# Output projection of chunk pairs by Strassen's seven products, in single steps spread over two iterations

## The chip, the cores and the metric

The kernel runs on one core of one Trainium2 chip. The metric is the device time of one execution in microseconds (us); lower is better. On the core, TensorE multiplies matrices (PE in the profile, its weight loads PEld), VectorE (DVE), ScalarE (ACT) and GpSimd (POOL) work on elements, and SyncE (SP) issues most of the transfers.

## The reference, cut to what matters

A layer on x of 2 x 1024 tokens with 512 columns, all in float32: an FFN with two experts (each token goes to one), an attention with a recurrent state of slots, and the same FFN again.

```python
x = x + 0.5 * _L0_ffn_ref(_layernorm(x), w_router, w_fc, w_proj)
x = x + _L0_attn_ref(_layernorm(x), Wq, Wk, Wv, Wg, Ws, Wo, g_norm_weight)
x = x + 0.5 * _L0_ffn_ref(_layernorm(x), w_router, w_fc, w_proj)

def _L0_attn_ref(hidden_states, ...):           # 16 heads, DK 64, DV 128, 64 slots
    q, k, v = (to_heads(hidden_states @ W) for W in (Wq, Wk, Wv))
    s = clip(to_heads(hidden_states @ Ws), -32, 32)
    o = _chunk_abc(q, k, v, s)                  # two scans over the tokens, softmax over slots between
    g = hidden_states @ Wg
    o = o * rsqrt(mean(o * o, -1) + 1e-5) * g_norm_weight
    o = o * (g * sigmoid(g))
    return o.reshape(b, t, 2048) @ Wo           # the output projection
```

## The kernel before

The first FFN (`Mixture`, `ffn`) sorts tokens by expert into blocks of up to 512 and runs six passes over them. The attention then runs as one loop over 64 units: two batches, four groups of four heads, eight chunks of 128 tokens, in this order from the outside in. The loop is a software pipeline: iteration i begins unit i (`cur`), does the softmax and the slot weights of unit i-1 (`mid`), and ends unit i-2 (`old`) with `transpose_out` and `project_out`. Even iterations begin an even chunk, odd ones an odd chunk. The last FFN's steps (`then_steps`) are drawn into the last iterations.

The order of TensorE's work in attention is fixed by hand: `on_pe` (L949 in the profile) makes each matmul issue behind the one before it. To have something to do while the softmax chain goes through VectorE and ScalarE, the loop calls `project` at set places; it takes steps of two generators, `values_gates` ("v") and `keys_slots` ("k"). These compute the projections of a pair of chunks together, by the seven products of Strassen's scheme (Winograd's form): four token sums X (`token_sums`) are made on VectorE, the weight sums were made beforehand on GpSimd (`weight_sums`, stored to HBM and loaded again by `load_values_gates` and `load_keys_slots`). A product is two matmuls of 128 x 128 by 256 or 512 columns; each float32 matmul has two records in the profile.

What the prediction speaks of, by name:

- Bp, svp, tk, ov, Ap, ok, ts, tu, `to` and skp are the PSUM tiles of a unit's own chain on TensorE: slot weights, state products, transposes of keys and slots, outputs, scores, slot scores, and the transposes around the softmax. B and A (L1106) are the masked copies of Bp and Ap that VectorE makes. CT is the running sum over slots (L1119) and rC its reciprocal (L1124). sq and ms lead to the norm's factor (L1208 to L1215), sg is the gate, and og the gated output. mx, e and rs are the softmax.
- `project_out` (tile `po`, L1261 for the add) multiplies a chunk's oT, four heads of 128 rows, by the group's 512 rows of Wo: four matmuls of 512 columns into one whole bank, then one VectorE add to the rows x.
- `keys_slots` has two tiles: kU (256 columns), and kV with halves C and V in one bank. kp, kv and ku are copies of partial sums to SBUF. It is drawn in five steps of two or one products.
- PSUM: tag `pj` has two buffers, for C and V of `values_gates`, for kU and kV, for the queries pq (made every fourth unit) and for po. Tag `st` is shared by ts, svp, skp, the rank's rp, and hC of the FFN. SBUF: all weights share the eleven buffers of `large_tile`, and sums the six of `sum_tile`.
- `feed` takes a finished row block into the last FFN's router. When enough have been fed it calls `rank` at once, which puts two small products (rp) on TensorE and scatters the rows.

Of the kernel before, what the change touches and what calls it, by code (L numbers as in the profile page):

```python
# [49 lines left out]
def tile_macaron(  # L50
# [55 lines left out]
    causal = const.tile([P, NPR, P], F32, tag="causal", name="causal")  # L106
    for h in range(NPR):
        nc.gpsimd.affine_select(
            out=causal[:, h, :],
            in_=ones,  # L110
            pattern=[[1, P]],
            compare_op=ALU.is_ge,
            fill=0.0,
            base=0,
            channel_multiplier=-1,
        )
# [4 lines left out]
    strict = const.tile([P, P], F32, tag="strict", name="strict")  # L121
    nc.gpsimd.tensor_tensor(strict, causal[:, 0, :], ident, ALU.subtract)
# [52 lines left out]
    vg_sums = [tc.dram_tile([P, 2 * 4 * 512], F32, name=f"vgs{g}") for g in range(NG)]  # L175
    ks_sums = [tc.dram_tile([P, 2 * 4 * 256], F32, name=f"kss{g}") for g in range(NG)]
# [8 lines left out]
    def layernorm_T(src, rows, xT, b, ph):  # L185
        for blk in range(2 * b, 2 * b + 2):
            xT[blk] = large_tile([P, DC, 512], f"xnT{ph}_{blk}")
            for j in range(4):
# [14 lines left out]
                nc.vector.tensor_scalar(xn, x, mv[:, 0:1], rstd, ALU.subtract, ALU.mult)  # L203
                tp = ps1.tile([P, DC, P], F32, tag="tr", name=f"ln{nm}")
# [27 lines left out]
    class Mixture:  # L232
# [3 lines left out]
        def __init__(self, ph, plan, split):  # L236
            self.ph, self.rows, self.split = ph, None, split
            self.passes, self.groups = plan
            self.starts = [sum(self.passes[:j]) for j in range(NPASS)]
            self.e1 = small_t([P, NT], "e1", f"e1{ph}")  # L240
            self.run = small_t([P, NT], "run", f"run{ph}")
            self.before = small_t([P, NT], "bef", f"bef{ph}")
            self.pos = small_t([P, NT], "pos", f"pos{ph}", mybir.dt.int32)

            self.own = small_t([P, NPASS], "own", f"own{ph}")
            self.seen = self.ranked = self.done = 0

        def feed(self):  # L250
# [12 lines left out]
            if self.seen == self.ranked + self.groups[self.done]:  # L263
                self.rank(self.groups[self.done])
                self.done += 1

        def rank(self, n):
# [14 lines left out]
            nc.tensor.matmul(rp[:, 0:n], lhsT=strict, rhs=e1[:, g], start=True, stop=False)  # L282
# [3 lines left out]
            V.tensor_tensor(r0, tokid[:, g], rp[:, 0:n], ALU.subtract)  # L286
            V.scalar_tensor_tensor(r1, rp[:, 0:n], float(REGION), r0, ALU.add, ALU.subtract)
# [164 lines left out]
    def ffn(m, views):  # L452
# [140 lines left out]
        def hidden_fast(ps, ck, xT, T, wfc, S, a, sums):  # L593
# [3 lines left out]
            for q in range(2):  # L597
# [18 lines left out]
                hA = work.tile([P, 512], F32, tag="oT", name=f"hA{nm}")  # L616
                hB = work.tile([P, 512], F32, tag="oT", name=f"hB{nm}")
# [216 lines left out]
    class Attention:  # L834
# [19 lines left out]
        def weight_sums(self):  # L854
# [18 lines left out]
            def load(j):  # L873
                g, d = j // 3, j % 3
                if d == 2:
                    return load_w(w_ks[g], f"kw{g}")
# [9 lines left out]
            for j in range(3 * NG):  # L886
                g, d = j // 3, j % 3
# [6 lines left out]
                else:  # L894
                    w = w.rearrange("p (k d n c) -> p k d n c", k=2, d=2, n=2)
                    parts = w[:, 0, :, 0], w[:, 0, :, 1], w[:, 1, :, 0], w[:, 1, :, 1]
                    to = ks_sums[g].rearrange("p (t d c) -> p t d c", t=4, d=2)
                    T = sum_tile([P, 3, 2, 256], f"K{g}")
                for i, _ in enumerate(sums(*parts, T)):
                    if i == 3:  # L900
                        store(to, T, parts[1])
                    if i == 1:
                        ahead = load(j + 1) if j != 2 and j + 1 < 3 * NG else None
# [18 lines left out]
        def load_keys_slots(self, b, g):  # L922
            nm = f"{b}_{g}"
            w = w_ks[g].rearrange("p (k d n c) -> p k d n c", k=2, d=2, n=2)
            B = sum_tile([P, 3, 2, 256], f"wks{nm}")
            for k in range(2):
                nc.sync.dma_start(out=B[:, k], in_=w[:, k, :, 0])
            T = large_tile([P, 4, 2, 256], f"ksT{nm}")
            nc.sync.dma_start(out=T, in_=ks_sums[g].rearrange("p (t d c) -> p t d c", t=4, d=2))
            nc.sync.dma_start(out=B[:, 2], in_=w[:, 1, :, 1])  # L930
            self.ks[b, g] = B[:, 0], B[:, 1], B[:, 2], T[:, 0], T[:, 1], T[:, 2], T[:, 3]
# [5 lines left out]
        def load_outputs(self, b, g):  # L937
            self.o[b, g] = load_w(w_o[g], f"wo{b}_{g}")

    def attention(att, then, then_steps, weight_steps):  # L940
# [83 lines left out]

        def keys_slots(u):
            pair = u, units[u.n + 1]
            B11, B21, B22, T1, T2, T3, T4 = att.ks[u.b, u.g]
            a11, a12, a21, a22 = halves(u)
            U = ps2.tile([P, 256], F32, tag="pj", name=f"kU{u.nm}")

            def keep(bank, tag):
                t = work.tile([P, 256], F32, tag=tag, name=f"{tag}{u.nm}", bufs=1)
                nc.scalar.copy(t, bank)
                return t
# [5 lines left out]
            def slot(v, bank, other):  # L1040
                v.E = work.tile([P, HG * M], F32, tag="E", name=f"E{v.nm}", bufs=3)
                nc.vector.tensor_tensor(v.E, bank, other, ALU.add)
                nc.vector.tensor_scalar(v.E, v.E, -32.0, 32.0, ALU.max, ALU.min)
                nc.scalar.activation(v.E, v.E, AF.Exp)

            product(U, a11, B11, True)
            p1 = keep(U, "kp")

            bank = ps2.tile([P, 2, 256], F32, tag="pj", name=f"kV{u.nm}")
            C, V = bank[:, 0], bank[:, 1]  # L1050
            product(C, a12, B21, True)
            nc.vector.tensor_tensor(key(u), C, p1, ALU.add)
            yield
            product(V, u.S[:, 0], T1, False)
            p5 = keep(V, "kv")
            product(U, u.S[:, 1], T2, False)
            u2 = keep(U, "ku")
            yield
            product(V, u.S[:, 3], B22, False)
            slot(u, V, u2)  # L1060
            yield
            product(U, u.S[:, 2], T3, False)
            slot(pair[1], U, p5)
            yield
            product(U, a22, T4, False)
            nc.scalar.copy(key(pair[1]), U)
            yield

# [24 lines left out]
        def masked_products(u, name, lT, rT):  # L1093
# [3 lines left out]
            for j in range(2):  # L1097
# [8 lines left out]
                nc.vector.tensor_tensor(m[:, ts(j, NPR), :], pp, causal[:, 0:NPR, :], ALU.mult)  # L1106
# [143 lines left out]
        def project_out(u):  # L1250

            tag = "at" if u.i >= NT - 3 and u.g == NG - 1 else "pj"
            pj = ps2.tile([P, D], F32, tag=tag, name=f"po{u.nm}")
            for h in range(HG):
                on_pe(
                    nc.tensor.matmul,
                    pj, lhsT=u.oT[:, h, :], rhs=att.o[u.b, u.g][:, ts(h, D)],
                    start=(h == 0), stop=(h == HG - 1),
                )
            x = rows[u.blk][:, u.c % 4, 0:D]  # L1260
            nc.vector.tensor_tensor(x, pj, x, ALU.add)  # L1261
            if u.g == NG - 1:
                then.feed()

# [16 lines left out]
        ahead = keys = None  # L1281
# [12 lines left out]
        for i in range(n + 2):  # L1294
            cur = units[i] if i < n else None
            mid = units[i - 1] if 1 <= i <= n else None
            old = units[i - 2] if i >= 2 else None


            def project(even, odd):  # L1300
                if i >= n - 1:
                    next(then_steps)
                for step in (odd if i % 2 else even) if cur else "":
                    if step == "v":
# [6 lines left out]
            project("k", "v")  # L1311
            if mid:
                slot_scores(mid)
            project("k", "v")
            if old:
                transpose_out(old)
            if mid:
                slot_softmax(mid)
            project("kvk", "v")
# [3 lines left out]
            project("vk", "v")  # L1323
# [7 lines left out]
            project("", "")  # L1331
            if cur and i % 2 == 0:
                ahead = None
            if mid:
# [3 lines left out]
                if mid.b == 0 and mid.c < 6 and mid.g < NG - 1:  # L1338
# [5 lines left out]
            if old:  # L1344
                project_out(old)
            if cur:
                if cur.g == NG - 1 and cur.b == 0:
                    next(norm)
                if cur.g == 0 and cur.b and cur.c in (1, 2):
                    att.load_rows(2 * cur.b + cur.c - 1)  # L1350

                if cur.c >= 4 and cur.n + NC < n:
# [7 lines left out]
                    else:  # L1360
                        att.load_outputs(v.b, v.g)
                if cur.g == NG - 1 and cur.b == B - 1:
                    if cur.c == 1:
                        then.lead_pass()
                    elif cur.c >= 3:

                        with tc.issue_after(mid.gated.ins):
                            next(then_steps)

# [9 lines left out]
    for ps, ck in ffn(first_mixture, x1_views):  # L1379
        if ps == NPASS - 1 and ck >= 2 and att.rows[ck - 2] is None:  # L1380
            att.load_rows(ck - 2)
        if ps == NPASS - 1 and ck == 3:
            with tc.issue_after(first_mixture.mark_dve.ins):
                next(norm, None)
            if (0, 0) not in att.vg:
# [3 lines left out]
        if ps == 2 and ck == 2:  # L1389
            for _ in range(min(3, 12 - done)):  # L1390
# [53 lines left out]
```

## Time and profile before

| What | us |
|---|---|
| median of 3 runs | 2368.47 |
| lowest and highest | 2363.77, 2371.63 |
| the profiled execution | 2368.13 |
| its span | 2366.4 |
| attention loop, from 535 to 1857 | 1322 |
| attention draining into the last FFN, 1857 to 1945 | 88 |

Each line of the profile's groups names the source line, the engine, the operation, the tile written and those read, the shape and count, then the busy time in us and the mean of one in ns, then the engine's idle time before them and what ended most of it. In the order of time a line has start and duration in us; matmuls of one kind in a row are merged. A matmul's record is about 0.17 us longer than the distance to the next one's start, since matmuls are pipelined; distances between starts are the better measure. Sums by stage list the window, its length, the busy time of PE, PEld, DVE, ACT and POOL with their counts, the granted TensorE clock as a share of full speed, and DMA.

### The profile page before, as it was taken

Reading aid. Unit: us, or ns where it says so; the run is one execution under the profiler, and the core shown is the slowest. Engines: PE = TensorE matmul, PEld = TensorE weight load, DVE = VectorE, ACT = ScalarE, POOL = GpSimd, SP = SyncE. Lnnn points to the kernel's source line nnn. Section 1 sums busy time; section 2 is a strip of 40 time slices with the busy share of each in tenths; the row PEclk is TensorE's granted clock in tenths of the full one; section 3 lists DMA queues with packets and bytes.
Section 4 is the critical chain, followed back from the end, with each engine's and each line's share of the span. In section 5 each row is a group of like instructions: output and inputs, shape, how many; then the busy total and the mean of one; then the engine's idle time right before and its main releaser. Section 6 shows DMA issues by size and latency. Waiting matters only on the chain.

```text
span 2366.4 us, 28341 instructions
## 1 busy us (share of the span) xinstructions
PE 2270.1 (96%) x10552; PEld 1566.4 (66%) x10552; DVE 1389.4 (59%) x3116; ACT 782.9 (33%) x1462; POOL 470.8 (20%) x401
## 2 busy tenths in 40 slices
PE   6999999999999999999999999999999989999998
PEld 5686787866656666665556666665665668888865
DVE  6553556557656656756666655655656666666411
ACT  2221222324334333343333343343433322222222
POOL 3613616101101101100101000000001244534000
PEclk9999999999999999999999999999999999999999
DMA  7516435221311411311301110111010104323442
GB/s 285 218 54 241 151 115 221 76 104 45 121 45 63 143 40 54 143 32 37 138 27 58 72 35 15 72 41 35 29 36 31 77 23 152 107 77 120 165 169 98
DMA packets 56938, 222.72 MB, mean 94 GB/s; under 512 B 5983, under 2 KB 13151, under 8 KB 38880
## 3 DMA queue, kind: packets, MB, share of 16 engines
q1 hardware_dynamic: 51232, 203.52, 24.1%
q0 software_dynamic: 5280, 16.85, 1.8%
q8 instruction: 84, 1.38, 0.2%
q14 instruction: 54, 0.44, 0.1%
q10 hardware_dynamic: 288, 0.52, 0.1%
HBM read 189.86 MB, written 31.54 MB: 94 GB/s over the span
## 4 chain that ended last, share of the span: by engine, by line
PE 75%; DVE 13%; issue 6%; ACT 2%; POOL 2%; DMA 1%; SPq 0%; POOLq 0%; DVEq 0%; ACTq 0%
PE U L949 9%; PE oa L673 6%; PE po L949 6%; PE hU L606 6%; PE pq L949 5%; PE o L673 5%; PE V L949 4%; PE kU L949 4%; PE hp L509 4%; PE kV L949 3%; PE hV L606 3%; PE op L728 3%; PE ov L949 3%; PE C L949 2%; DVE rC L1124 2%
## 5 line engine op out<-in xcount | busy, mean ns | idle before, releaser
L1217 POOL TENSOR_TENSOR sg<-sg,ms 128x512 f32<-128x512 f32 x64 | 67.6, 1056 | 1248.6 <-DVE ms L1215 1209.1
L949 PE MATMUL po<-wo,oT 128*128 128x512 f32 x512 | 238.4, 609 | 1.7 <-DVE A L1106 1.7
L949 PEld LDWEIGHTS po<-wo,oT 128*128 128x128 f32 x512 | 92.6, 191 | 102.4 <-issue 93.0
L509 PE MATMUL hp<-xsT,wfc 128*128 128x256 f32 (+1 forms) x768 | 149.8, 350 | 10.3 <-DMA wfc<-in_w_fc_dram 5.6
L509 PEld LDWEIGHTS hp<-xsT,wfc 128*128 128x128 f32 x768 | 128.0, 193 | 33.6 <-issue 13.9
L728 PE MATMUL op<-wp,a 128*128 128x512 f32 x320 | 143.2, 593 | 0.0
L1213 ACT ACT_TABLE_LOAD x64 | 82.1, 1283 | 157.1 <-DVE ms L1212 157.0
L496 DVE SCALAR_TENSOR_TENSOR t<-hp,r 128x256 f32<-128x256 f32 (+1 forms) x96 | 36.3, 378 | 153.7 <-ACT r L495 151.7
L949 PE MATMUL U<-vgT,X 128*128 128x512 f32 x256 | 120.3, 592 | 0.0
L949 PE MATMUL pq<-xnT,wq 128*128 128x512 f32 x256 | 112.5, 592 | 0.0
L1124 DVE RECIPROCAL rC<-CT 128x256 f32<-128x256 f32 x64 | 111.4, 1740 | 0.6
L606 PE MATMUL hU<-xsT,wfc 128*128 128x256 f32 x384 | 100.2, 383 | 0.9 <-ACT e L613 0.9
L728 PEld LDWEIGHTS op<-wp,a 128*128 128x128 f32 x320 | 59.7, 190 | 60.9 <-issue 57.4
L1106 DVE TENSOR_TENSOR A<-Ap,causal 128x256 f32<-128x256 f32 x128 | 53.1, 420 | 54.6 <-PE Ap L949 53.1
L495 ACT ACTIVATE r<-hp 128x256 f32<-128x256 f32 (+1 forms) x96 | 33.3, 348 | 155.3 <-PE hp L509 151.0
L949 PEld LDWEIGHTS pq<-xnT,wq 128*128 128x128 f32 x256 | 47.4, 190 | 53.6 <-issue 53.6
L606 PEld LDWEIGHTS hU<-xsT,wfc 128*128 128x128 f32 x384 | 72.2, 191 | 14.2 <-issue 3.0
L1156 ACT ACT_TABLE_LOAD x63 | 80.8, 1283 | 1.2
L949 PEld LDWEIGHTS U<-vgT,X 128*128 128x128 f32 x256 | 48.6, 190 | 47.6 <-issue 45.9
L995 ACT ACTIVATE th<-sg 128x512 f32<-128x512 f32 x64 | 40.4, 631 | 109.4 <-DVE sg L993 102.4
L1219 DVE TENSOR_TENSOR og<-ov,sg 128x512 f32<-128x512 f32 x64 | 44.2, 690 | 52.0 <-POOL sg L1217 52.0
L1248 ACT ACTIVATE oT<-to,gnh 128x512 f32<-128x512 f32 x64 | 44.0, 687 | 92.4 <-PE to L949 80.7
(296 smaller groups left out, 5087.8 us busy)
## 6 DMA issues: line engine op xcount, KB each, us to landing
wfc<-in_w_fc_dram SPq DMA_DIRECT2D x48, 1024.0 KB, 5.6
wp<-in_w_proj_dram SPq DMA_DIRECT2D x48, 1024.0 KB, 6.9
vgT<-vgs SPq DMA_DIRECT2D x16, 1024.0 KB, 5.3
wv<-in_w_v_dram SPq DMA_DIRECT2D x8, 1024.0 KB, 7.7
ksT<-kss SPq DMA_DIRECT2D x8, 1024.0 KB, 4.9
wo<-in_w_o_dram SPq DMA_DIRECT2D x8, 1024.0 KB, 4.8
xs<-xs SPq DMA_DIRECT2D x6, 1032.0 KB
wks<-in_w_ks_dram SPq DMA_DIRECT2D x24, 256.0 KB, 4.2
```

The lines of the kernel that those rows point to most:

```text
L509: m.mark = nc.tensor.matmul(hp, lhsT=wfc[:, dc * HQ + hc * P : dc * HQ + (hc + 1) * P], rhs=xT[:, dc, :], start=(dc == 0), stop=(dc == DC ...
L606: m.mark = nc.tensor.matmul(bank, lhsT=left[:, d, :], rhs=right[:, d, :], start=start and d == 0, stop=d == 1, skip_group_check=True,)
L673: nc.tensor.matmul(bank[:, t, :], lhsT=left(q)[:, ts(t, P)], rhs=right(q), start=first and q == 0 and (t == 0 or last), stop=last and q == ...
L728: nc.tensor.matmul(ops[j], lhsT=a[hc][:, ts(j, P)], rhs=wp[:, ts(hc, D)], start=(ck == 0 and hc == 0), stop=(ck == NHQ - 1 and hc == HQ // ...
L949: att.pe = op(*args, **kw)
L1106: nc.vector.tensor_tensor(m[:, ts(j, NPR), :], pp, causal[:, 0:NPR, :], ALU.mult)
L1124: nc.vector.reciprocal(u.rC, u.CT)
L1156: nc.scalar.activation(u.u, u.u, AF.Exp)
L1213: nc.scalar.activation(ms, ms, AF.Sqrt, bias=eps, scale=1.0 / DV)
L1217: u.gated = then.gated = nc.gpsimd.tensor_tensor(sg, sg, ms.to_broadcast([P, HG, DV]), ALU.mult)
L1219: nc.vector.tensor_tensor(u.og, op, sg, ALU.mult)
L1248: nc.scalar.activation(u.oT, tp, AF.Copy, scale=gnh)
```

## The change

The output projection of two neighbouring chunks u and w becomes one generator of seven steps ("o" in `project`). Each step is one product into a half of a single bank, followed by a VectorE add of that half to the rows. Step 1 closes the even iteration in which u is `old`; steps 2 to 5 lie in the odd iteration; steps 6 and 7 lie in the next even one. The token sums are made by `out_sums` on VectorE in the odd iteration. Sums of Wo are made on GpSimd beside the others and loaded with B11, B21 and B22 of Wo at a group's second unit. Keys and slots become seven steps too, with both halves U and V in one bank. The rank of the last FFN is deferred to `settle`, called at one place of an iteration; the layernorm of the second batch is cut in two, so that its transposes come one call after its rows are normalized; the causal mask is kept once and broadcast; hA and hB of the FFN move to other tags; the loop has one iteration more.

```diff
+        def settle(self):
+            while self.done < len(self.groups) and self.seen >= self.ranked + self.groups[self.done]:
+                self.rank(self.groups[self.done])
+                self.done += 1
...
                 nc.vector.tensor_scalar(xn, x, mv[:, 0:1], rstd, ALU.subtract, ALU.mult)
+                yield
                 tp = ps1.tile([P, DC, P], F32, tag="tr", name=f"ln{nm}")
...
-            for j in range(3 * NG):
-                g, d = j // 3, j % 3
+            for j in range(4 * NG):
+                g, d = j // 4, j % 4
...
         def load_outputs(self, b, g):
-            self.o[b, g] = load_w(w_o[g], f"wo{b}_{g}")
+            self.o[b, g] = self.load_halves(w_o[g], o_sums[g], f"o{b}_{g}")
...
         def keys_slots(u):
+            bank = ps2.tile([P, 2, 256], F32, tag="pj", name=f"kU{u.nm}")
+            U, V = bank[:, 0], bank[:, 1]
...
+            product(V, a12, B21, True)
+            nc.scalar.copy(key(u), V)
+            yield
             product(U, a11, B11, True)
+            nc.vector.tensor_tensor(u.k, U, u.k, ALU.add)
+            yield
+            product(U, u.S[:, 1], T2, False)
+            nc.scalar.copy(slot(u), U)
+            yield
...
+        def project_out(u):
+            w = units[u.n + 1]
+            B11, B21, B22, T1, T2, T3, T4 = att.o[u.b, u.g]
...
+            last = u.n >= n - 4
+            bank = (ps1 if last else ps2).tile([P, 2, 256], F32, tag="ok" if last else "pj", name=f"po{nm}")
+
+            def add(i, v, k):
+                x = rows[v.blk][:, v.c % 4, ts(k, 256)]
+                V.tensor_tensor(x, bank[:, i], x, ALU.add)
+
+            a11, a12 = u.oT[:, 0:2], u.oT[:, 2:4]
+            product(bank[:, 1], a12, B21, True)
+            add(1, u, 0)
+            yield
+            product(bank[:, 0], a11, B11, True)
+            add(0, u, 0)
+            yield
+            a21, a22 = w.oT[:, 0:2], w.oT[:, 2:4]
+            product(bank[:, 0], w.S[:, 1], T2, False)
+            add(0, u, 1)
+            yield
+            product(bank[:, 1], w.S[:, 0], T1, False)
+            add(1, w, 1)
+            yield
+            product(bank[:, 1], w.S[:, 3], B22, False)
+            add(1, u, 1)
+            feed(u)
+            yield
+            product(bank[:, 0], w.S[:, 2], T3, False)
+            add(0, w, 1)
+            yield
+            product(bank[:, 0], a22, T4, False)
+            add(0, w, 0)
+            feed(w)
+            yield
+
+        def out_sums(u, w):
...
+            V.tensor_tensor(S[:, 0], a21, a22, ALU.add)
+            V.tensor_tensor(S[:, 1], S[:, 0], a11, ALU.subtract)
+            V.tensor_tensor(S[:, 3], a12, S[:, 1], ALU.subtract)
+            V.tensor_tensor(S[:, 2], a11, a21, ALU.subtract)
...
-            project("k", "v")
+            project("kok", "vo", 1)
             if mid:
                 slot_scores(mid)
-            project("k", "v")
+            project("kok", "v")
...
             if old:
                 transpose_out(old)
+                if i % 2:
+                    out_sums(units[i - 3], old)
             if mid:
                 slot_softmax(mid)
-            project("kvk", "v")
+            project("kvk", "v", 1)
...
-            project("vk", "v")
+            project("vk", "ov", 1)
+            with tc.issue_after(att.pe.ins):
+                then.settle()
...
-            project("", "")
+            project("", "o")
...
                 outputs(mid)
                 update_value_state(mid)
...
             if cur:
                 scores(cur)
-            if old:
-                project_out(old)
+            if old and i % 2 == 0:
+                outs = project_out(old)
+            project("o", "o")
...
+                if cur.c == 1 and (cur.b, cur.g) not in att.o:
+                    att.load_outputs(cur.b, cur.g)
```

The third argument of `project` is the number of `then_steps` that it takes once the last unit has begun; before, each of the five calls took one.

## The prediction

> **What bounds the kernel now.** I read the table of busy time first, then the sums by stage, then the groups by shape, then who waited for whom on TensorE, and last the order of time of two neighbouring units.
>
> ```profile
> PE 2270.1 (96%) x10552; PEld 1566.4 (66%) x10552; DVE 1389.4 (59%) x3116; ACT 782.9 (33%) x1462; POOL 470.8 (20%) x401
> ...
> 535.00:1857.00 1322.00, 1291.61 (x6259) 799.44 (x6258) 831.42 (x1980) 515.17 (x848) 131.59 (x117) 1.00 0.17 60
> 1857.00:1945.00 88.00, 76.23 (x360) 55.41 (x359) 55.60 (x122) 25.60 (x49) 26.36 (x23) 0.92 0.11 44
> ```
>
> The attention loop runs from 535 to 1857 us; TensorE is idle in 30 us of it, VectorE busy in 63%. So time can be gained there only by giving TensorE less to do, and is lost by every new wait of TensorE. The last 88 us, where attention drains into the last FFN, hold 12 us of idleness and a lowered clock (0.92).
>
> ```profile
> L949 PE MATMUL po<-wo,oT 128*128 128x512 f32 x512 | 238.4, 609 | 1.7 <-DVE A L1106 1.7
> L949 PEld LDWEIGHTS kU<-ksT,X 128*128 128x128 f32 x256 | 49.0, 194 | 20.2 <-issue 15.1 <-ACT e L1156 0.2
> ...
> PE kV L949 <- DVE k L1052: 13.4, 20, 1.8
> PE rp L282 <- DVE e L273: 4.7, 3, 1.6
> ```
>
> The third line is the one to remember. `kV` writes columns 256 to 511 of a PSUM bank, the VectorE add `k` reads columns 0 to 255 of it, and TensorE waits for that add: what is tracked is the bank, not its halves. The changed kernel puts its new products into halves of one bank.
>
> ```profile
> 916.09 3.70 PE L949 MATMUL po<-wo,oT 128*128 128x512 f32 x8
> 919.63 1.03 PE L949 MATMUL kU<-wks,xnT 128*128 128x256 f32 x4
> 920.57 1.13 PE L949 MATMUL kV<-wks,xnT 128*128 128x256 f32 x4
> 921.54 0.61 PE L949 MATMUL ok<-qT,sk 128*128 128x128 f32 x4
> ...
> 914.41 0.86 DVE L1119 TENSOR_TENSOR_SCAN CT<-ones,CT,kET 128x128 f32<-128x128 f32 x2 [0.29 <-ACT kET L1091]
> 915.18 0.39 DVE L1241 TENSOR_TENSOR sv<-svp,sv 64x256 f32<-64x256 f32 x1
> 915.50 1.74 DVE L1124 RECIPROCAL rC<-CT 128x256 f32<-128x256 f32 x1
> 917.16 0.62 DVE L1210 TENSOR_REDUCE ms<-sq 128x4 f32<-128x512 f32 x1
> 917.81 0.43 DVE L1241 TENSOR_TENSOR sv<-svp,sv 64x256 f32<-64x256 f32 x1
> 918.27 0.16 DVE L1211 TENSOR_TENSOR ms<-ms,rs 128x4 f32<-128x4 f32 x1
> 918.47 0.42 DVE L1106 TENSOR_TENSOR A<-Ap,causal 128x256 f32<-128x256 f32 x1
> 918.81 0.15 DVE L1212 TENSOR_TENSOR ms<-ms,rs 128x4 f32<-128x4 f32 x1
> 918.88 0.42 DVE L1106 TENSOR_TENSOR A<-Ap,causal 128x256 f32<-128x256 f32 x1
> 919.83 0.69 DVE L1261 TENSOR_TENSOR x<-po,x 128x512 f32<-128x512 f32 x1 [0.54 <-PE po L949]
> ```
>
> At the end of each unit VectorE works without a gap from 914.41 to 919.30, with a reciprocal of 1.74 us in the middle; this costs nothing today because `po` holds TensorE for 3.54 us meanwhile. The adds to the rows come last in that row.
>
> **The change part by part.** The sum is made against the profiled execution's own time, 2368.1 us (span 2366.4 and 1.7 around it); the median of the runs, 2368.5, is the same.
>
> *Fewer columns on TensorE.* `po` has 16 records for a pair of chunks. Starts of neighbouring 512-wide records lie 0.429 us apart, of 256-wide ones 0.2155 (a product of four records, 0.86: kU to ts in any unit). So 16 x 0.429 = 6.86 us become 7 x 4 x 0.2155 = 6.03: 0.83 us a pair, x32 pairs = **-26.6 us**. Row against rule: a 256-wide product loads weights as often as a 512-wide one, so a pair goes from 16 loads to 28 of 0.19 us. The Trainium skill ("TensorE: Matmul & The Clock Gate", the section on the mechanism of row and column tiling) says that weight loads overlap running matmuls only when their row groups differ; these all use the full 128 rows. By it the 12 loads more would cost 2.3 us a pair, and the term would be +46. The trace disagrees: the starts are 0.2155 apart with a load of 0.19 between each two, so they do overlap. I take the trace.
>
> *Waits that go.* `kV`'s first product waits today for a buffer that the add of `po` frees: 0.94 instead of 0.86 behind `kU`, and 0.97 instead of 0.86 inside: 0.19 x 32 = **-6**. Keys in seven steps have as many evictions as before; the wait of 13.4 us for `k` remains between the same two neighbours (a product, the scores, a product), but with VectorE earlier through its queue I let **-5** of it go.
>
> *New waits of the single steps.* Each of the seven steps must wait for the VectorE add of the step before it. Most steps lie 2 us or more apart. Two do not. (1) From an odd to an even iteration: step 5 closes the odd one, and step 6 follows after only one key product. From Bp at 911.86: ov, with step 4 put before it, and Ap end at 4.23 + 0.86 = 5.09; step 5 takes 0.96 (0.10 more as the first after narrow products, as `po` with its 3.54 shows), the key product 0.86: step 6 could start at 6.91. VectorE's second A ends at 7.44 now (919.30); the add of step 4 is in front of it (+0.34, the spacing of two neighbours), so 7.78; the add of step 5 takes it to 8.1, and step 6 starts at 8.2: **1.3 us**, x32 = 41.6. I put this add behind A because A stands before it in the program and is ready earlier. (2) From an even to an odd iteration without queries the same count gives step 2 at 4.24 + 0.96 + 1.72 (U) = 6.92, and the add of step 1 done at 7.44 + 0.34 + 0.07 = 7.85: 0.93, x16 = 14.9. With queries, every second time, 6.9 us of query products cover the reciprocal: 0. Together **+56.5**. Queued behind the waiting step on TensorE are the second key product and the slot scores, so the softmax chain moves with it. Bounds: 0 (the adds go ahead of the reciprocal) and 115 (they go behind ms L1214, which ended at 920.84, 1.2 us later in each of 48 places).
>
> *A buffer held longer.* The output bank now lives from the end of one even iteration to the next, so C and V of values and gates share the other `pj` buffer. V starts 0.65 us after C's last product (C to `to` to `ts` to V); the add that empties C needs about 0.2 + 0.69 + 0.07. So 0.35 x 31 = **+11** (0 to 20).
>
> *VectorE's added work.* A pair gets seven adds of 0.42 for two of 0.69, and four sums `out_sums` of about 0.43, 0.43, 0.43 and 0.72 (the X rows): +3.6 us of some 43. Apart from the places above it lies where VectorE idles (1.0 to 1.8 us at a time before `mx`, `rs` and `B`); the softmax's `e` goes back by 0.4, under the table load of 1.28 that ACT spends before its exp. Nothing; 0.3 us a pair, 10 us, if that cover is gone.
>
> *Rank, layernorm split, the end.* The deferred rank moves two small products behind work that is queued: up to 4.7 of `rp`; the layernorm's transposes come an iteration after their rows are ready: 2.2 (`ln`) and part of 2.8 (`to`). I take -7. The last 88 us lose 12 us in waits and 7 in clock; fewer FFN steps and more single steps fill them, one more iteration drains: -8, between -20 and +10. Together **-15**.
>
> *Loads and sums of the output weights.* Sixteen POOL additions more (1.27 to 1.44 us), four loads and twelve stores more, and three more issues on SP for each of the eight groups. The loads now start at a group's second unit, over 20 us before the first use (wo lands 4.8 us after issue); the sum tile can wait there for a buffer, with the later loads of SP behind it, and its first use is step 3, some 15 us further on. Four of the POOL sums fall into the first FFN's third pass, where POOL makes no other sums. **+2** (0 to 8). The tag moves of hA and hB, and the smaller causal mask (same 0.42 row), nothing: the VectorE queue already orders their reuse.
>
> Sum: -26.6 - 6 - 5 + 56.5 + 11 - 15 + 2 = +17, so **2385 us**.
>
> **The rivals.** *It gets faster:* the adds are done in time. Then the 56.5 is gone: 2385 - 56.5 = 2329. It decides once the 48 waits average less than 0.83 us (the other terms sum to -39.6) instead of 1.18. For it: VectorE is idle in 37% of the stage, and the scheduling may see a cheaper reciprocal. Against it: the order of adds above. *VectorE becomes the bound:* the adds go behind the ms chain, 2385 + 58 = 2443; against it, today's `x` stands before L1214. *It cancels:* waits of 0.8 us each, 2368 give or take 7.
>
> **How the numbers follow.** Waits of about 1.2 us: 0.50, with 2370 to 2405 for its own range; adds in time: 0.25; VectorE bound: 0.14; cancelled: 0.11. A measurement of this kernel tells about 0.3%, 7 us, from no change. Faster by more than that: the second case and a little of the first, 0.27; within: 0.12; slower: 0.61. The range takes in most of the fast case and part of the slow one: 2330 to 2428.
>
> **What would show it.** `po` in 256-wide records of 0.2155 us spacing, 896 of them; a new line in TensorE's waits, `po` for the VectorE add `x`, of 40 to 60 us in some 48 places, just behind the reciprocal in time; V waiting for `v` L1005 by about 10 us; `rp` no longer waiting. If the line of `po` for `x` is under 20 us, I am wrong and the kernel is faster; if it is over 100, the third case holds. Starts of `po` records further apart than 0.22 us without a wait would say that the weight loads count after all.

## The result, and the profile after

The changed kernel takes 2440.46 us, the median of 4 runs (2436.02 to 2443.86); the kernel before takes 2369.09 beside it. The ratio is 1.0303, with a 95% interval from 1.0278 to 1.0329. The forecast was 2385, with a range to 2428: the direction was right, the size was not. By the medians 71.4 us were added, by the profiled executions (spans of 2442.2 and 2366.4) 75.8; the one of the changed kernel was the slowest of its four. The tables below go by the profiled executions. The runs of one kernel spread over 3 to 14 us, so a difference of a few us between two single executions says little.

First the busy times, then the sums by stage of the kernel after; the stages are cut at the same points of the work as those shown of before (window, length, PE, PEld, DVE, ACT, POOL, granted clock, DMA).

```profile
PE 2270.6 (93%) x10936; PEld 1634.6 (67%) x10936; DVE 1458.8 (60%) x3415; ACT 782.5 (32%) x1466; POOL 491.2 (20%) x415
...
543.00:1888.00 1345.00, 1249.47 (x6390) 834.81 (x6388) 863.25 (x2168) 497.95 (x823) 135.82 (x119) 0.99 0.19 65
1888.00:1975.00 87.00, 81.53 (x447) 58.05 (x447) 60.50 (x167) 30.95 (x53) 15.93 (x14) 0.98 0.20 73
```

In the attention stage TensorE's busy time fell from 1291.6 to 1249.5 us, and its idle time grew from 30 to 96. The work did become less; the waits took it back and more. The last 87 us have 5.5 us of idleness where before had 12, and a clock of 0.98 for 0.92.

The groups by shape, for the new products and for their weight loads:

```profile
L957 PE MATMUL poo<-To,so 128*128 128x256 f32 x384 | 103.9, 394 | 38.3 <-DVE x L1088 34.0
...
L957 PEld LDWEIGHTS poo<-To,so 128*128 128x128 f32 x384 | 66.6, 193 | 56.6 <-DVE x L1088 46.4
```

And who waited for whom on TensorE (total us, times, longest):

```profile
PE poo L957 <- DVE x L1088: 44.5, 47, 2.0
PE tu L957 <- ACT e L1218: 22.3, 31, 0.7
PE kU L957 <- DVE k L1059: 16.2, 23, 2.2
...
PE hp L515 <- DMA wfc<-in_w_fc_dram: 11.3, 2, 9.6
...
PE V L957 <- DVE v L1013: 5.8, 29, 0.2
```

The first line is the wait that was forecast, in 47 places (48 were forecast); 45 of them lie in the loop, 30 ahead of step 6 and 15 ahead of step 2. The second was not forecast at all. The third should have shrunk from 14 us and did not. The fourth stood at 5.6 before.

**The ledger.** The loop from the first unit's Bp to the 63rd's can be split without a remainder: to each product on TensorE I charge the time from its start to the start of whatever comes next, so a wait is charged to the product ahead of it. (us, summed over the loop; e9 and e7 are experiments further on.)

| product | before | after | e9 | e7 |
|---|---|---|---|---|
| output projection | 215.8 | 201.7 | 196.5 | 192.8 |
| U of values and gates | 210.5 | 250.6 | 252.0 | 223.1 |
| V and C of values and gates | 163.2 | 169.0 | 167.5 | 163.1 |
| keys and slots | 207.0 | 240.3 | 211.8 | 203.5 |
| ok (slot scores) | 88.9 | 83.6 | 69.6 | 67.4 |
| ts | 13.7 | 25.5 | 25.5 | 14.8 |
| all others | 439.7 | 440.9 | 441.5 | 432.4 |
| loop | 1338.8 | 1411.6 | 1364.4 | 1297.1 |
| ahead of the loop | 535.9 | 543.8 | 541.7 | 539.6 |
| behind it | 491.7 | 486.8 | 483.8 | 482.7 |

Of the 72.8 us by which the loop grew, 40.1 are charged to U and 33.3 to the keys. U contains two waits: step 2's for the add of step 1 (12.7 above its usual distance), and that of `tu`, which stands behind U in odd iterations, for the exp (26.8). The keys contain step 6's wait for the add of step 5 (38.7); without it they are 5.4 below before. ts holds V's late start (10.7 of its 11.8; the rest is one wait of the FFN). The new products themselves need 852 records at 0.2155 = 183.6 us, against 488 at 0.429 = 209.4 before; that is the forecast saving. But their 201.7 lie 18.1 above it, where before's lay 6.4 above. Two things are in the 18.1. In 17 places the key product that follows waits for ScalarE's copy k and starts 1.26 us after the step instead of 0.97: 5.0 us, which are gone in e9 (12.9 above) and e7 (9.2 above). The other 13.1 are late starts: what follows a step that itself came after a wait, or after Ap or ok, starts about 0.1 us late, and seven pieces have more such edges than one.

**Where steps 5 and 6 meet.** The order of time in the even unit whose Bp starts at 943.81, on TensorE, then VectorE, then ScalarE:

```profile
948.91 1.13 PE L957 MATMUL poo<-wo,so 128*128 128x256 f32 x4
949.88 1.03 PE L957 MATMUL kU<-wks,xnT 128*128 128x256 f32 x4
951.96 1.13 PE L957 MATMUL poo<-To,so 128*128 128x256 f32 x4 [1.05 <-DVE x L1088]
953.22 1.13 PE L957 MATMUL kU<-wks,xnT 128*128 128x256 f32 x4
954.19 0.61 PE L957 MATMUL ok<-qT,sk 128*128 128x128 f32 x4
...
955.97 1.13 PE L957 MATMUL kU<-Tks,X 128*128 128x256 f32 x4 [0.58 <-DVE k L1059]
...
951.15 0.42 DVE L1168 TENSOR_TENSOR A<-Ap,causal 128x256 f32<-128x256 f32 x1
951.49 0.41 DVE L1088 TENSOR_TENSOR x<-poo,x 128x256 f32<-128x256 f32 x1
...
954.89 0.69 DVE L1281 TENSOR_TENSOR og<-ov,sg 128x512 f32<-128x512 f32 x1 [0.93 <-POOL sg L1279]
955.50 0.41 DVE L1059 TENSOR_TENSOR k<-kU,k 128x256 f32<-128x256 f32 x1
...
951.32 1.28 ACT L1275 ACT_TABLE_LOAD   x1 [2.35 <-DVE ms L1274]
952.61 0.30 ACT L1275 ACTIVATE ms<-ms,eps 128x4 f32<-128x4 f32 x1
952.81 0.35 ACT L1056 COPY k<-kU 128x256 f32<-128x256 f32 x1
```

Step 5 starts 5.10 us after Bp (forecast 5.09), the second A ends at 7.76 (7.78), the add x at 8.09 (8.1), step 6 starts at 8.15 (8.2). That chain held to a tenth of a microsecond, and the others are like it: the 45 steps start 7.75 to 8.47 us after Bp, but for one at 9.10. What I did not follow is the key chain behind it. The first key product was done by 950.9, but its copy to SBUF stands in ScalarE's order behind the square root of ms with its table load, and runs at 952.81; so the second key product starts at 953.22, 0.3 us late. Its add on VectorE stands behind og, which waits for GpSimd; so the third key product is 0.58 us late as well. Three waits follow each other in one stretch, and the list of waits can only show what was left of each.

Step 6, and the second key product too, write one half of a bank while the add or the copy that they wait for reads the other half. No run gives the halves banks of their own, so whether these waits would go by that alone is not known.

**Where the exp was lost.** In the odd unit before it, VectorE and then ScalarE, after:

```profile
935.84 0.41 DVE L1215 TENSOR_REDUCE mx<-ts 128x4 f32<-128x256 f32 x1
936.32 0.42 DVE L1122 TENSOR_TENSOR so<-oT 128x256 f32<-128x256 f32 x1
936.66 0.42 DVE L1125 TENSOR_TENSOR so<-oT,oT 128x256 f32<-128x256 f32 x1
937.00 0.42 DVE L1123 TENSOR_TENSOR so<-so,oT 128x256 f32<-128x256 f32 x1
937.33 0.42 DVE L1217 TENSOR_TENSOR e<-ts,mx 128x256 f32<-128x256 f32 x1
...
938.05 0.58 ACT L993 COPY p<-V 128x512 f32<-128x512 f32 x1 [1.77 <-PE V L957]
938.65 1.28 ACT L1218 ACT_TABLE_LOAD   x1
939.95 0.42 ACT L1218 ACTIVATE e<-e 128x256 f32<-128x256 f32 x1
```

and the same place before:

```profile
906.16 0.41 DVE L1153 TENSOR_REDUCE mx<-ts 128x4 f32<-128x256 f32 x1
906.61 0.42 DVE L1155 TENSOR_TENSOR e<-ts,mx 128x256 f32<-128x256 f32 x1
...
906.63 1.28 ACT L1156 ACT_TABLE_LOAD   x1
907.92 0.42 ACT L1156 ACTIVATE e<-e 128x256 f32<-128x256 f32 x1
908.25 0.57 ACT L985 COPY p<-V 128x512 f32<-128x512 f32 x1
```

Three sums of o stand between mx and e, so e is about 1 us later. That alone would not matter: e is done at 937.75, and ScalarE has been idle for 1.77 us. With the load beside e the exp would end near 938.2 (an estimate from these rows), and tu's place on TensorE comes only at 939.5. But the order of ScalarE's instructions is fixed when the kernel is built, and with the later e the copy p of V came ahead of the table load and the exp: in 30 of the 64 units after, in none before. So the table load, which used to run beside e, waits for TensorE's V. From the start of mx to the end of the exp it was 2.18 us before and is 4.53 now. The Trainium skill ("PSUM — Partial Sum Buffer", section "Engine vs sequencer instructions") says that ScalarE's queue is strictly first in, first out; the trace agrees: the exp's operand lay ready for 0.9 us while the load stood behind p.

### The profile page after: what moved, and what is told of

Its sections match the earlier page's. It is cut to its first block, busy times and chain, and to the rows that moved or that the text cites. A ratio compares the mean times of both kernels' runs of the same rounds, so it can differ in the third digit from the quotient of the medians.

```text
span 2442.2 us, 29465 instructions
## 1 busy us (share of the span) xinstructions
PE 2270.6 (93%) x10936; PEld 1634.6 (67%) x10936; DVE 1458.8 (60%) x3415; ACT 782.5 (32%) x1466; POOL 491.2 (20%) x415
## 4 chain that ended last, share of the span: by engine, by line
PE 61%; DVE 16%; issue 12%; ACT 4%; POOL 3%; DMA 2%; SPq 0%; POOLq 0%; DVEq 0%; another core or an unknown queue 0%; ACTq 0%
PE kU L957 7%; PE oa L679 6%; PE U L957 5%; PE hU L612 5%; PE o L679 4%; PE pq L957 4%; PE poo L957 4%; PE V L957 4%; PE hp L515 3%; PE op L734 3%; PE hV L612 3%; DVE rC L1186 2%; PE C L957 2%; PE hC L612 1%; PE ok L957 1%
## 5 line engine op out<-in xcount | busy, mean ns | idle before, releaser
L957 PE MATMUL poo<-To,so 128*128 128x256 f32 x384 | 103.9, 394 | 38.3 <-DVE x L1088 34.0
L1088 DVE TENSOR_TENSOR x<-poo,x 128x256 f32<-128x256 f32 x224 | 93.5, 417 | 50.8 <-PE poo L957 50.0
L957 PE MATMUL kU<-Tks,X 128*128 128x256 f32 x384 | 103.3, 391 | 17.4 <-DVE k L1059 16.2
L957 PEld LDWEIGHTS poo<-To,so 128*128 128x128 f32 x384 | 66.6, 193 | 56.6 <-DVE x L1088 46.4
L957 PEld LDWEIGHTS kU<-Tks,X 128*128 128x128 f32 x384 | 70.5, 191 | 47.7 <-DVE k L1059 22.1
```

Source lines behind the costliest of these rows:

```text
L957: att.pe = op(*args, **kw)
L1088: V.tensor_tensor(x, bank[:, i], x, ALU.add)
```

## The experiments

The times are medians; the ratio is to the kernel before, run on the same chip, with its 95% interval. Beside e1 to e4 the kernel before had a median of 2364.11 us, beside e5 to e8 2366.61, beside e9 to e12 2369.85; steps between these groups are therefore compared by the loop's length in the profile (1411.6 after, 1338.8 before).

### The two orders, alone and together

*e1_step_before_scores*: steps 1 and 5 ahead of the scores.

```diff
+            if old and i % 2 == 0:
+                outs = project_out(old)
+            project("o", "o")
             if cur:
                 scores(cur)
-            if old and i % 2 == 0:
-                outs = project_out(old)
-            project("o", "o")
```

> The closing step of each iteration (step 5 in odd ones, step 1 in even ones) and its add are issued before the scores Ap and their masked copies A, not behind them; the work is the same. Theory (the step that follows waits for an add that stands last in VectorE's queue): the add of step 5 ends about 6.8 to 7.1 us after Bp instead of 8.1, the waits of the output steps for the add x fall from 44.5 us to under 15, and the time from 2440 to about 2395. Rival (VectorE is simply too busy at the end of an iteration, whatever the order): the wait moves to A, the slot scores ok wait for A by about as much, and the time stays within 10 us of 2440. The wait of tu for the softmax's exp stays at 22 us in both.

Measured: 2413.49 us, ratio 1.0206 (1.0183 to 1.0229), loop 1386.1. The wait for x fell from 44.5 to 14.3 us as expected, but kU's wait for ScalarE's k copy (L1056) rose from 1.4 to 18.5. The loop became 25.5 us shorter, not 45.

*e2_sums_after_softmax*: the sums of o behind the softmax.

```diff
             if old:
                 transpose_out(old)
-                if i % 2:
-                    out_sums(units[i - 3], old)
             if mid:
                 slot_softmax(mid)
+            if old and i % 2:
+                out_sums(units[i - 3], old)
```

> The four token sums of the output projection (out_sums) are issued behind the softmax's max and subtraction instead of before them; the work is the same. Theory (three of these sums stand before the subtraction e, so ScalarE takes the copy p of values and gates before the exp with its table load, and tu waits): the 22 us of tu waiting for exp fall to under 3, the time falls by 25 to 30 us to about 2413, and the waits of the output steps for x stay at 44 us. Rival (the exp is late for another reason, the table load of 1.28 us itself): tu still waits, the time stays within 8 us of 2440.

Measured: 2403.24 us, ratio 1.0162 (1.0141 to 1.0183), loop 1378.5, 33.1 shorter. `tu` no longer waits (0.4 us in one place). The odd unit of e2, VectorE and ScalarE:

```profile
926.45 0.43 DVE L1122 TENSOR_TENSOR so<-oT 128x256 f32<-128x256 f32 x1
926.79 0.42 DVE L1217 TENSOR_TENSOR e<-ts,mx 128x256 f32<-128x256 f32 x1
...
926.44 1.28 ACT L1218 ACT_TABLE_LOAD   x1
927.73 0.42 ACT L1218 ACTIVATE e<-e 128x256 f32<-128x256 f32 x1
928.18 0.58 ACT L993 COPY p<-V 128x512 f32<-128x512 f32 x1
```

One sum is still ahead of e, and hides under the table load, just as the forecast had it; the table load is back ahead of p. The copy p of V stands ahead of the exp in no unit any more. VectorE does the same work as in the changed kernel. The cost was the order, not the sums.

*e3_both_orders*: both edits.

> Both moves together. If the two causes are separate places of TensorE's queue they add up: about 45 + 28 us, so about 2368, level with the kernel before. Rival (one stretch of VectorE's queue behind both): the second move brings less than half of what it brings alone, and the time is above 2385.

Measured: 2383.4 us, ratio 1.0078 (1.0056 to 1.0101), loop 1357.0. The two gains nearly add up (25.5 + 33.1 = 58.6; 54.6 measured), yet the kernel stays behind before, where 2368 was expected. Its waits:

```profile
PE kU L957 <- ACT k L1056: 18.8, 25, 1.0
PE poo L957 <- DVE x L1088: 14.4, 31, 0.9
...
PE kU L957 <- DVE k L1059: 7.7, 19, 1.2
```

*e4_cheap_reciprocal*: the reciprocal of the running sum replaced by a multiplication by zero and the addition of a constant, so that the division is left out and the operation takes 0.28 us in place of 1.74.

```diff
-            nc.vector.reciprocal(u.rC, u.CT)
+            nc.vector.tensor_scalar(u.rC, u.CT, 0.0, 1e-12, ALU.mult, ALU.add)
```

> The changed kernel with the reciprocal of the running sum (1.74 us of VectorE in each unit) replaced by a fused multiply and add that writes a constant; the division by the running sum is left out. Theory (the step waits are VectorE's backlog behind the reciprocal): a 256-wide SBUF operation takes about 0.3 us, so everything behind it comes 1.4 us earlier; the waits of the output steps for x fall from 44.5 to under 10 us, and the time falls by 45 us or more. Rival (the wait is the latency of a single add and not the queue): the waits for x stay above 30 us.

Measured in one run: 2404.61 us, loop 1374.1, 37.5 shorter. The wait for x is down to 1.6 us, so the reciprocal is what made the adds late. But here, too, the k copy came out from behind it:

```profile
PE kU L957 <- ACT k L1056: 26.0, 30, 1.3
```

That is at least a part of why the gain stayed under the 45 us expected.

### Removing the waits one after another

*e5_key_step_early*: e3, and the first key step of the next pair is taken in the odd iteration, right after step 4.

```diff
-            if cur and i % 2 == 0:
-                keys = keys_slots(cur)
-            project("kok", "vo", 1)
+            if i == 0:
+                keys = keys_slots(cur)
+                next(keys)
+            project("ko", "vo", 1)
...
             project("", "o")
+            if i % 2 and i + 1 < n:
+                keys = keys_slots(units[i + 1])
+                next(keys)
```

> e3_both_orders with one more edit: the first of the seven key steps of the next pair runs in the odd iteration right after step 4 of the output projection, ahead of step 5, so that ScalarE's copy of its product (L1056) is in the queue well ahead of the square root of ms and its table load. Theory (the wait of kU for that copy, 18.8 us in e3, is what stood behind the step wait, and the key chain is what holds TensorE from step 5 to the slot scores): kU's wait for ScalarE falls below 4 us, poo's wait for x (14.4) and kU's wait for VectorE's k (7.7) fall by half, e3's 2383 becomes about 2350 to 2358. Rival (the stretch is bound by VectorE's reciprocal and the A adds, whoever waits first): the idle time turns up at another product, step 5 or the second key step, and the time stays above 2375.

Measured: 2339.72 us, ratio 0.9894 (0.9879 to 0.991), loop 1311.2. It gained more than expected (45.8 in the loop): kU's waits are 0.9 for ScalarE and 1.7 for VectorE, and poo waits 0.3 us for x in one place. The wait did not turn up elsewhere. This kernel is 1.1% faster than before.

*e6_c_product_first*: e5, and of the two products whose sum is v the one in C comes first.

```diff
-            product(U, a11, B11, True)
-            p1 = keep(U, "th", "p1")
-            token_sums(u)
-            yield
             C = ps2.tile([P, 512], F32, tag="pj", name=f"C{u.nm}")
             product(C, a12, B21, True)
             u.v = out("v", u)
-            nc.vector.tensor_tensor(u.v, C, p1, ALU.add)
+            nc.scalar.copy(u.v, C)
+            token_sums(u)
+            yield
+            product(U, a11, B11, True)
+            nc.vector.tensor_tensor(u.v, U, u.v, ALU.add)
```

> e5_key_step_early with the two products of values and gates that share an output changed in order: C's product first, emptied by ScalarE into v, then U's, added to it by VectorE, so that C's buffer is free before V asks for it. Theory (V is late by 0.35 us an iteration because it waits for the add that empties C): V's wait for v disappears, 10 to 14 us less than e5. Rival (the 0.35 us is taken back by the next wait, tu for the exp or U for its operands): within 5 us of e5.

Measured: 2327.26 us, ratio 0.9835 (0.9819 to 0.9851), 12.5 below e5, and V's wait for v is gone.

*e7_wo_sums_split*: e6, and the fourth of the sums of Wo is made in FFN pass 4 in place of pass 2.

```diff
-                        ahead = load(j + 1) if j != 3 and j + 1 < 4 * NG else None
+                        ahead = load(j + 1) if j not in (2, 3) and j + 1 < 4 * NG else None
...
-        if ps == 2 and ck == 2:
-            for _ in range(min(4, 16 - done)):
+        if ck == 2 and ps in (2, 4):
+            for _ in range(min(3, 12 - done) if ps == 2 else min(1, 16 - done)):
```

> e6_c_product_first with the fourth of the sums of Wo made in FFN pass 4 instead of pass 2 (no load ahead of it in pass 2). Theory (in the head the load of wfc comes late because the fourth sum's load of Wo stands ahead of it): hp's wait for wfc goes back from 10 to 12 us to about 5.6, the head (start to first Bp) from 541 to 544 to about 536 to 538, the time falls by 4 to 6 us against e6. Rival (the late load is the three other sums' doing, or a queue's state): head unchanged. If both theories of e5 and e6 hold too, this kernel comes to about 2335 and beats both kernels.

Measured: 2324.44 us, ratio 0.9828 (0.9814 to 0.9842). hp's wait for wfc is back at 5.6 us, and it is 3.7 and 6.2 in e10 and e11, which have the same edit, against 9.5 to 12.4 without it; so the cause of that wait was found. The saving was not: the head came to 539.6, 3.7 above before, and the median fell by 2.8, with intervals that overlap. The head is 541.4 to 546.7 in all runs without the edit, 539.6 to 543.6 in the three with it and 535.9 and 536.6 in the two of before, so by their means (543.2, 541.0, 536.3) about a third of the difference is explained, and the rest is open. Who waits for whom on TensorE in e7:

```profile
PE hp L515 <- DMA wfc<-in_w_fc_dram: 5.6, 3, 3.7
...
PE poo L957 <- DVE x L1088: 0.3, 1, 0.3
```

It beats both kernels: 42 us under before, 116 under the change as it was made.

*e8_projection_as_before*: the changed kernel with the old projection, the sums of Wo still made but not read.

```diff
+            for h in range(HG):
+                on_pe(
+                    nc.tensor.matmul,
+                    pj, lhsT=u.oT[:, h, :], rhs=att.o[u.b, u.g][:, ts(h, D)],
+                    start=(h == 0), stop=(h == HG - 1),
+                )
...
+            nc.vector.tensor_tensor(x, pj, x, ALU.add)
...
-            project("kok", "vo", 1)
+            project("kk", "v", 1)
-            project("kok", "v")
+            project("kk", "v")
```

> The changed kernel with the output projection as before (four 512-wide matmuls a chunk on the whole Wo, one add of 512 columns, no sums of o), the rest kept: keys in seven steps, deferred rank, split layernorm, and the sums of Wo still made and stored but not read. Theory (the single steps of the projection and VectorE's sums for them are what cost 71 us): about 2355 to 2370, as before, with kU's wait for ScalarE's copy below 5 us because po holds TensorE meanwhile. Rival (keys in seven steps cost by themselves): above 2385, with the waits of kU for k growing.

Measured: 2388.38 us, ratio 1.0105 (1.0086 to 1.0124), loop 1362.0. My theory missed and the rival was right: the keys in seven steps cost by themselves.

```profile
PE kU L957 <- ACT k L1056: 21.6, 32, 1.9
...
PE kU L957 <- ACT E L1062: 14.3, 31, 0.5
...
PE kU L957 <- DVE k L1059: 7.0, 15, 0.9
```

These are 43 us of waits where the old keys had 14. Without the output steps the key steps follow each other directly, and each waits for the eviction of the one before it. This run doesn't tell what the keys cost in the changed kernel, where output steps stand between most of them. It does say that the seven key steps need other work between them; the output steps with the keys as before were not run. A rule of the Trainium skill ("Perfetto Trace Analysis", "Matmuls") bears on it: independent groups of matmuls should go through different banks, so that the emptying of one lies beside the next. e8 fits it for 36 of the 43 us, the waits for ScalarE's copies (L1056 and L1062), which read the half that the next product does not write; the 7.0 for k are for the half that is written. e7 limits it: there all seven output products go through one bank, and wait 0.3 us for each other's adds in all, since other work stands between any two of them.

### One edit alone, and one left out

*e9_key_step_early_alone*: the changed kernel with the key step's edit of e5 and nothing else.

> The changed kernel with one edit only: the first key step of the next pair runs in the odd iteration right after step 4, ahead of outputs; step 5 stays behind the scores, the sums of o stay ahead of the softmax. Theory (three waits stand one behind another between step 5 and the slot scores: poo for x, kU for k, and the late exp elsewhere; removing one shows the next): kU's wait for k (16.2 us) falls below 4, poo's wait for x (44.5) stays at 40 to 48, tu's wait for the exp (22.3) stays, so 2440 becomes about 2420 to 2428. Rival (the early key step gives the 46 us in any surroundings, as it took off 44 us in e5): about 2395, with poo's wait for x gone.

Measured: 2394.65 us, ratio 1.0116 (1.009 to 1.0142), loop 1364.4, 47.2 shorter. I had expected the wait for x to stay; the rival's time was met exactly, though over a third of that wait is left:

```profile
PE tu L957 <- ACT e L1218: 22.7, 31, 0.7
PE poo L957 <- DVE x L1088: 16.9, 28, 0.7
```

The order of time, in the unit whose Bp starts at 928.71, shows why:

```profile
934.67 1.13 PE L957 MATMUL poo<-wo,so 128*128 128x256 f32 x4
935.64 1.03 PE L957 MATMUL kU<-wks,xnT 128*128 128x256 f32 x4
936.64 1.13 PE L957 MATMUL poo<-To,so 128*128 128x256 f32 x4
937.61 0.61 PE L957 MATMUL ok<-qT,sk 128*128 128x128 f32 x4
...
936.17 0.42 DVE L1088 TENSOR_TENSOR x<-poo,x 128x256 f32<-128x256 f32 x1
...
932.37 0.37 ACT L1056 COPY k<-kU 128x256 f32<-128x256 f32 x1 [1.14 <-PE kU L957]
```

Step 6 starts 7.93 us after Bp, little earlier than in the changed kernel (8.15). VectorE's chain through the reciprocal sets that time either way. But now both key products are done by then, and not one: the work that used to stand behind the wait has been moved into it. And ScalarE copies k at 932.37, ahead of the square root and its table load. The slot scores start at 8.90 after Bp; they started at 10.38.

*e10_all_but_step_order*: e7 without the edit of e1.

> e7_wo_sums_split with step 1 and step 5 of the output projection put back behind the scores, as in the changed kernel. Theory (the forecast's step waits, 56 us, were right and are worth their price once nothing else stands behind them): poo's wait for x comes back with 25 to 45 us, and the time is 2324 + 40 to 50 = 2364 to 2374, no better than before. Rival (with the key step early the gap between step 5 and 6 no longer holds TensorE): within 10 us of 2324.

Measured: 2344.91 us, ratio 0.9912 (0.9883 to 0.9941), loop 1321.1, 24.0 above e7. The wait for x is 16.7 us, as in e9. With the key step early, what the order of the steps still buys is, for 12.7 of the 24.0 us, the wait between steps 1 and 2 (in odd units without queries step 2 starts mostly 2.62 us after the wide product ahead of it, as in the changed kernel; the product needs 1.72), and for 7.7 what is left of the wait between steps 5 and 6. The expected 40 to 50 was too much.

*e11_all_but_sums_order*: e7 without the edit of e2.

> e7_wo_sums_split with the four sums of o put back ahead of the slot softmax. Theory (they push e behind the copy p on ScalarE, so that table load and exp come late in every odd iteration, 0.73 us and a restart, 31 times): tu's wait for the exp comes back with 22 us, and the time is 2324 + 26 to 37 = 2350 to 2361. Rival (the late exp is hidden behind the other waits and costs only when they are there): within 10 us of 2324.

Measured: 2353.47 us, ratio 0.9938 (0.9917 to 0.9959), loop 1326.0, 28.9 above e7, with `tu` waiting 20.1 us for the exp. The late exp costs about the same whether other waits are there or not (33.1 in e2).

*e12_before_c_product_first*: the kernel before with the edit of e6.

> The kernel before with one edit, that of e6: C's product of values and gates first, emptied by ScalarE into v, then U's, added by VectorE. It asks whether the 12 us of e6 belong to the change's buffer or would have come in any case. Theory (V waits for C's buffer only because the output bank holds the other one from iteration to iteration): no gain here, 2360 to 2370. Rival (the order itself saves work or a wait): 2350 to 2357.

Measured: 2369.08 us, ratio 0.9995 (0.9985 to 1.0005). No effect: the 12.5 us of e6 belong to the change's use of the buffers.

## Why the prediction was wrong

Each term of its sum, in us, against what the ledger shows (the waits for k and of rp and lt stand behind ok and are charged to it in the ledger):

| step of the prediction | forecast | measured |
|---|---|---|
| fewer columns on TensorE | -26.6 | -25.8 by spacing; +6.7 for late starts |
| a key product's wait for ScalarE's copy k, behind an output step | none | +5.0 |
| V, C, Ap and Bp | none | +7.8 (2.9 of late starts, 4.9 of small waits) |
| waits that go (kV's buffer, k) | -11 | -3.7 (-5.4 and, for k, +1.7) |
| new waits of the single steps | +56.5 | +51.4 (38.7 and 12.7) |
| a buffer held longer (V) | +11 | +11.8 (10.7 at V) |
| VectorE's added work | 0 | +28.6 (26.8 at `tu`, 1.8 behind it) |
| rank, layernorm split, the end | -15 | -14.5 (rp -4.9, lt -2.0, ln -2.7, end -4.9) |
| loads and sums of Wo | +2 | +7.9 (all that is ahead of the loop) |
| left over in single groups | none | +0.6 |
| sum | +17 | +75.8 |

**The step that failed** is "VectorE's added work": "the softmax's `e` goes back by 0.4, under the table load of 1.28 that ACT spends before its exp. Nothing". I named the right cover, and 10 us if it was gone. But I moved e by one sum where three got ahead of it, and took for granted that the table load would stay where it was. The load is itself an entry in ScalarE's order; with e later, p went ahead of it. That is half of what was missed (28.6 of 58.8 us): e2 takes 33.1 us off the changed loop, e11 puts 28.9 back on the best one.

**Late starts** are another miss, 9.6 us together (6.7 and 2.9): I had counted 0.10 us for steps 1 and 5 alone, and nothing in the sum, while each of the seven products, and what follows it, can pay it.

**The keys** are a third, 12.3 us: their terms sum to +1.3 (-3.7 and 5.0) where -11 was forecast. "VectorE earlier through its queue" was to bring 5 us of the k wait; it went from 14.0 to 16.2. VectorE was not the whole chain: ScalarE's copy stands behind a table load, and og behind GpSimd. e1, e3 and e4 showed the wait for that copy as 18.5 to 26 us once the wait ahead of it was shortened.

Of the loads, I had asked what waits for Wo; the cost came from what Wo's load stands ahead of, a load of wfc in the head (e7). That accounts for the longer wait of hp; of the 7.9 us, e7 leaves 3.7 or more unexplained.

**What held.** The spacing of narrow products, with weight loads of 0.193 us beside them: the output projection costs less than before wherever no key product waits long behind it, 192.8 to 201.9 against 215.8 (in e1, e3 and e4, with that wait charged to it, 216 to 224). So the trace was the better guide than the sentence on row groups. The same section of the Trainium skill ("TensorE: Matmul & The Clock Gate", "The mechanism") also lets a load into a background weight buffer be pulled ahead, which the prediction left out; the trace does not contradict that. The step waits came where they were forecast, 38.7 us for 41.6 and 12.7 for 14.9. V's late start, the rank and the layernorm came in about their sizes.

The first rival, a faster kernel at 2329, named the adds being in time as its condition. That is what e5 to e7 bring about, and they end at 2324 to 2340, though with the other waits removed as well, so the nearness of the number does not test its sum. The second rival gave 2443, close to the measured time, but by another mechanism: the adds did not go behind the ms chain. Its nearness is chance.

## What to carry to other kernels

On a nearly saturated engine, follow a wait to the end of its stretch: list what is next late on every queue, for the longest wait hides those behind it, and removing it alone returns only the difference. Before adding work to one engine, check whether a later result changes the built order on another; a table load that leaves its place can cost more than the work that pushed it (here the exp ended 2.35 us later because its operand came 1 us later). Where a wait ends at a time set by another engine's chain, move work from behind the wait to ahead of it before shortening that chain: moving one key product did here (47 us) what a reciprocal six times faster did not (37.5).

## What was not expected of the hardware

A product of four 256-wide records takes 0.86 us to the next start, and 0.97 when it comes after a wait, or after Ap or ok; after tk and skp, which are as narrow, it takes 0.87, and after the wide U sometimes the one and sometimes the other, so what decides it is open. Over the loop the output projection's late starts came to 13.1 us with 852 records, and to 6.4 with 488. The granted clock of the loop's stage was 1.00 before and 0.99 after, so this is not the clock.
